# Softmax values of an attention layer: how many query groups are transposed by DMA, and where the softmax sums are divided out

## The chip, the cores and the metric

The kernel runs on one core of a Trainium2 chip. The metric is the device time of one execution in microseconds (us). The engines are TensorE (PE, with its weight loads PEld), VectorE (DVE), ScalarE (ACT), GpSimd (POOL) and SyncE (SP, which here only issues DMAs).

## The reference, cut to what matters

Four layers on x of 4 x 1024 x 256 in fp32, each added to x: a linear recurrent layer, a gated sparse feed-forward layer (ffn), attention with 8 heads of 64, and the same ffn again. The change is in the attention layer:

```python
q = (x @ Wq.T).reshape(b, t, 8, 64)
kv_latent = x @ Wkv_down.T
k = (kv_latent @ Wk_up.T).reshape(b, t, 8, 64)
v = (kv_latent @ Wv_up.T).reshape(b, t, 8, 64)
scores = jnp.einsum('bqhd,bkhd->bhqk', q, k) * 64 ** -0.5
attn = jax.nn.softmax(scores, axis=-1)
out = jnp.einsum('bhqk,bkhd->bqhd', attn, v).reshape(b, t, 512)
x = x + out @ Wo.T
```

x is layer-normalized before each layer. The weights Wk_up and Wv_up are folded into those of the queries and of the output, so that keys and values are both the latents of a batch (64 numbers for each of 1024 tokens).

## The kernel before, in words

**Stages.** The program has three stages after each other: the recurrent layer (c1 in the code), attention together with most of the first ffn (c2), and the second ffn (c3). In the attention part, the function `heads` is the main line, and `merge` (L952) places the steps of other generators between its steps, by due times counted in steps of `heads`. The instructions are recorded in this order, and then placed on the engines' queues by the builder with a model of their times (`schedule_with_timeline_sim`, L1298). Each engine works through its queue in order.

**The main line.** `heads` (L856) goes over 4 batches (one call for each, L1193), 2 blocks `nb` of 512 queries, 4 head pairs `g` and 4 groups `q` of 128 queries: 128 pairs of (group, head pair). A pair has two steps, one for each head `j`, which makes 64 steps a batch (`STEPS`). One step does this:

- scores (L881): four products of 128 x 512 on TensorE, high and low halves of the latents, into the PSUM buffer `sc`, 128 x 1024 (two buffers);
- the negated maximum `nm` (L885) on DVE, straight from `sc`;
- `pr` = exp(sc + nm) on ACT (L889, three buffers), which also sums each row into `ssum`.

Then the 128 x 1024 of `pr` have to be transposed, since the value product needs keys on the partitions. There are two ways:

- groups 0 and 2 (`by_dma`, L864): `nm` is shifted by 11 ln 2 on DVE (L887), ACT casts `pr` to fp16 (L892), POOL writes the remainder `pr - pd` as a second fp16 half (L893), and SP issues a DMA transpose of both halves, 128 x 2048 (L894), from `pd` (two buffers) into `d0` or `d1` (two buffers of each).
- groups 1 and 3: eight 128 x 128 transposes on TensorE (L900) into PSUM, and two copies of 128 x 512 by ACT (L905), or one by DVE (L903) in the last batch, into `p0` and `p1`.

**Value sums.** `values_sum` (L915) multiplies the transposed probabilities with the latents for both heads of a pair: 16 products in fp32 for the TensorE way (TensorE shows two instructions for each), 48 in fp16 for the DMA way, where each of 8 blocks of keys has three terms. They are called some steps later: that of a TensorE pair in the next pair's first step, that of a DMA pair in the second step of the next DMA pair. Each call also divides by the softmax sums: a reciprocal of `ssum` on DVE (L919), a broadcast of it to 64 columns a head on POOL (L921), a transpose of that on TensorE (L933), a copy to `rb` on ACT (L935), and a multiplication into `on` on DVE (L936). Its PSUM buffer `po` has the tag "s", of which there are two, shared with everything that `merge` places beside the main line.

**Output.** `output` (L938) runs for a block of 512 queries after its four head pairs, once for each of 4 groups: `on` for all heads (128 x 512) is split in a high half on ACT (L945) and a low half on POOL (L946), 12 products go to PSUM (L947), and DVE adds them to x (L948).

**Beside it.** `merge` also places 24 tiles of the first ffn (`Ffn.tile` with `fine=True`, in seven steps each), which use `ex`, `wk` and `xg` with two buffers each (L609, L610, L654); the queries (L842), the latents of the next batch (L782), and the second ffn's `head` (L501), which needs the x that `output` has written. After the main line, the last two groups' output and half a `head` run bare (L1194).

Of the kernel before, what the change touches and what calls it, by code (L numbers as in the profile page):

```python
# [487 lines left out]
class Ffn:  # L488
# [100 lines left out]
    def tile(self, i, sp, psum, tags, out=None, fast=False, parts=None, tt=None, fine=False):  # L589
# [18 lines left out]
        ssum = sp.tile([P, 2], F32, tag="ssum", name="ssum")  # L608
        ex = sp.tile([P, 2, D], F32, tag="ex", name="ex")  # L609
        wk = sp.tile([P, 2, D], F32, tag="wk", name="wk")  # L610
        for s in range(2):
# [161 lines left out]
class Attention:  # L773
    def __init__(self, tc, x, ident, ident64, wqk, wvo, wd, sp, wp):
        self.nc, self.x, self.ident, self.ident64 = tc.nc, x, ident, ident64
        self.wqk, self.wvo, self.wd, self.sp, self.wp = wqk, wvo, wd, sp, wp
        self.hp = None
        self.k, self.xnt, self.qs, self.on = {}, {}, {}, {}

        self.sident = wp.tile([HD, HD], F32R, tag="sident", name="sident")  # L780
# [74 lines left out]

    def heads(self, b, psum):  # L856

        nc, sp, wp = self.nc, self.sp, self.hp  # L860
        kh, kl, la, lb = self.k[b]
        late, pending = [], []
        for nb, g, q in ((nb, g, q) for nb in range(2) for g in range(PAIRS) for q in range(4)):
            by_dma = q % 2 == 0  # L864
            if g == 0:
                self.on[b, nb, q] = wp.tile([P, PAIRS, P], F32, tag=f"on{q}", name=f"on{q}")
            qs = self.qs[b, nb, g]
            ssum = sp.tile([P, 2], F32, tag="ssum", name="ssum", bufs=4)
            if by_dma:
                pts = [wp.tile([P, 2 * TPB, P], F16, tag=f"d{j}", name=f"d{j}", bufs=2) for j in range(2)]  # L870
                parts = ((0, lb[0]), (TPB, lb[0]), (0, lb[1]))
                terms = [(v[:, c, :], i + c) for c in range(TPB) for i, v in parts]
            else:
                pts = [wp.tile([P, TPB, P], F32, tag=f"p{j}", name=f"p{j}") for j in range(2)]
                terms = [(la[:, c, :], c) for c in range(TPB)]
            for j in range(2):
# [11 lines left out]
                pr = wp.tile([P, T], F32, tag="pr", name="pr", bufs=3)  # L888
                nc.scalar.activation(pr, sc, AF.Exp, bias=nm, accum_out=ssum[:, j : j + 1])  # L889
                if by_dma:  # L890
# [20 lines left out]
            (late if by_dma else pending).append((pts, terms, ssum, self.on[b, nb, q][:, g, :]))  # L911
        for args in late + pending:
            self.values_sum(*args, psum)

    def values_sum(self, pts, terms, ssum, on, psum):  # L915

        nc, sp = self.nc, self.sp
        rs = sp.tile([P, 2], F32, tag="rs", name="rs")
        nc.vector.reciprocal(rs, ssum)  # L919
        rows = sp.tile([P, 2, HD], F32, tag="rows", name="rows")  # L920
        nc.gpsimd.tensor_copy(rows, rs[:, :, None].to_broadcast([P, 2, HD]))  # L921
        po = psum.tile([P, 2, P], "s", "pmo")
        for n, (v, c) in enumerate(terms):
            for j in range(2):
                nc.tensor.matmul(  # L925
                    po[j * HD : (j + 1) * HD, 0, :],
                    v,
                    pts[j][:, c, :],
                    start=(n == 0),
                    stop=(n == len(terms) - 1),  # L930
                )

        nc.tensor.transpose(po[:, 1, :], rows.rearrange("p j d -> p (j d)"), self.ident)  # L933
        rb = sp.tile([P, P], F32, tag="rb", name="rb", bufs=1)
        nc.scalar.copy(rb, po[:, 1, :])  # L935
        nc.vector.tensor_tensor(on, po[:, 0, :], rb, ALU.mult)  # L936

    def output(self, b, nb, psum, tiles=range(4)):  # L938

        nc = self.nc  # L940
        for q in tiles:
            xt = self.x[b * TPB + nb * 4 + q]
            py = psum.tile([P, D], "s", "pmy")
            on = [self.hp.tile([P, PAIRS, P], F32R, tag=f"onp{i}", name=f"onp{i}") for i in range(2)]
            nc.scalar.copy(on[0], self.on[b, nb, q])  # L945
            nc.gpsimd.tensor_tensor(on[1], self.on[b, nb, q], on[0].bitcast(F32), ALU.subtract)  # L946
            products(nc, py, [([t[:, g, :] for t in on], [t[:, g, :] for t in self.wvo]) for g in range(PAIRS)])  # L947
            nc.vector.tensor_tensor(xt, xt, py, ALU.add)  # L948
            yield
# [79 lines left out]
def tile_kernel(ctx: ExitStack, tc: tile.TileContext, x_in, w_lru, vecs_in, rows, w_ffn, lin_t, w_attn, w_down, out):  # L1029
# [88 lines left out]
    with ExitStack() as c2:  # L1118
# [53 lines left out]
        for b in range(B):  # L1172
            n = STEPS * b
# [8 lines left out]
            side.append((n + 40 if b == B - 1 else n + STEPS + 24, f2.head(2 * b, sp, psum, "s"), 2))  # L1182
            last = b == B - 1
            side.append((n + STEPS if last else n + STEPS + 8, f2.head(2 * b + 1, sp, psum, "s", (0,) if last else (0, 1)), 1 if last else 2))
# [117 lines left out]
```

## Time and profile before

| What | us |
|---|---|
| median of 3 runs | 1536.99 (1534.27 to 1539.68) |
| the profiled execution's own time | 1533.81 |
| its span | 1532.1 |
| busy in the span: PE, PEld | 1297.4, 960.2 |
| busy in the span: DVE, ACT, POOL | 1182.9, 1014.5, 681.6 |
| DMA transposes | 128, on the queue q1 with 88.50 MB |

The span is cut in 40 slices of 38.3 us below. A digit is the busy share of an engine in a slice in tenths, and 9 is 90% or more; PEclk is the clock granted to TensorE in tenths of full speed.

```
PE   4879998698898898898998889888999998657786
[...]
DVE  8976665697887878887778687777676675499998
ACT  5353433664787777787787777877777776476664
[...]
PEclk9999999698999999999999999999999999789888
DMA  3010000331454334344433345434444454000000
```

The attention stage with its DMA transposes runs from slice 11 to slice 34. A row of a group by line has the line, engine, operation, what it writes and reads, shapes and count; then busy time and the mean duration of one in ns; then the engine's idle time just before, with what ended most of it. A row of the waits has who waited for whom, and then the total in us, how many times, and the longest. A row of the busy times by stretch has, for each engine, its busy us and in brackets its number of instructions.

### The profile page before, as it was taken

What the parts mean: (1) busy time and instruction counts of PE and PEld (TensorE: products, weight loads), DVE (VectorE), ACT (ScalarE), POOL (GpSimd) and SP (SyncE); (2) the same over time, 40 slices, a digit from 0 to 9 for tenths busy, and PEclk for the clock granted to TensorE, in tenths of its full rate; (3) what the DMA queues carried; (4) which work ended last, traced back from release to release, by engine and by line L of the source; (5) the groups of instructions that cost most, each with busy time, mean ns of one, the idle gap of its engine ahead of it and who ended that gap; (6) DMA issues with size and microseconds to landing.
All of it is one profiled execution on the core that took longest, in us unless ns stands there. A gap on an engine that the chain in (4) does not pass through costs nothing. (4 is left out here: it accounts for less than half of the span.)

```text
span 1532.1 us, 28693 instructions
## 1 busy us (share of the span) xinstructions
PE 1297.4 (85%) x10136; PEld 960.2 (63%) x10136; DVE 1182.9 (77%) x3674; ACT 1014.5 (66%) x2145; POOL 681.6 (44%) x848
## 2 busy tenths in 40 slices
PE   4879998698898898898998889888999998657786
PEld 3635455365676766766776767677777776334554
DVE  8976665697878887878778687777676675499998
ACT  5353433664787777787777787877777776476664
POOL 2033333162545454544543554454443534157776
PEclk9999999698999999999999999999999999789888
DMA  3010000331454334344433345434444454000000
GB/s 117 32 41 15 21 21 14 135 101 44 76 91 90 70 70 80 67 80 77 85 76 60 65 85 81 66 60 85 78 75 88 83 95 83 1 11 24 25 25 28
DMA packets 288609, 96.51 MB, mean 63 GB/s; under 512 B 268233, under 2 KB 284626, under 8 KB 288466
## 3 DMA queue, kind: packets, MB, share of 16 engines
q1 hardware_dynamic: 283024, 88.50, 29.0%
q10 hardware_dynamic: 5442, 6.18, 1.2%
q8 instruction: 80, 1.31, 0.3%
q14 instruction: 63, 0.52, 0.1%
HBM read 16.01 MB, written 11.53 MB: 18 GB/s over the span
## 5 line engine op out<-in xcount | busy, mean ns | idle before, releaser
L893 POOL TENSOR_TENSOR pd<-pr,pd 128x1024 f16<-128x1024 f32 x128 | 273.5, 2142 | 256.5 <-ACT pd L892 198.6
L885 DVE TENSOR_REDUCE nm<-sc 128x1 f32<-128x1024 f32 x256 | 308.5, 1218 | 76.8 <-PE sc L881 75.3
L889 ACT ACTIVATE pr<-sc,nm 128x1024 f32<-128x1024 f32 x256 | 285.9, 1120 | 89.8 <-DVE nm L887 53.3
L881 PE MATMUL sc<-kh,qs 128*128 128x512 f32 x512 | 184.9, 439 | 27.1 <-ACT pr L889 19.5
L881 PE MATMUL sc<-kl,qs 128*128 128x512 f32 x512 | 162.4, 398 | 0.0
L674 DVE MATCH_REPLACE8 wk<-m,wk 128x256 f32<-128x256 f32 x384 | 158.3, 419 | 0.1
L905 ACT COPY p<-ptp 128x512 f32<-128x512 f32 x224 | 124.3, 590 | 46.3 <-PE ptp L900 38.2
L900 PE MATMUL ptp<-ident,pr 128*128 128x128 f32 x1024 | 140.2, 277 | 15.6 <-ACT pr L889 14.8
L674 DVE MAX8 m<-wk 128x8 f32<-128x256 f32 x384 | 153.0, 424 | 0.4
L925 PE MATMUL pmo<-p,la 128*64 128x128 f32 x2048 | 142.3, 287 | 5.6 <-ACT ft L524 2.9
L900 PEld LDWEIGHTS ptp<-ident,pr 128*128 128x128 f32 x1024 | 117.1, 141 | 38.0 <-ACT pr L889 24.9
L892 ACT CAST pd<-pr 128x1024 f16<-128x1024 f32 x128 | 133.3, 1055 | 5.9 <-DMA d<-pd 4.8
L925 PEld LDWEIGHTS pmo<-p,la 128*64 128x64 f32 x2048 | 121.5, 143 | 24.2 <-ACT ft L524 5.1
L881 PEld LDWEIGHTS sc<-kh,qs 128*128 128x128 f32 x512 | 85.6, 196 | 51.9 <-ACT pr L889 30.8
L881 PEld LDWEIGHTS sc<-kl,qs 128*128 128x128 f32 x512 | 97.1, 190 | 23.4 <-issue 1.4
L925 PE MATMUL pmo<-d,lb 128*64 128x128 f16 x3072 | 101.8, 221 | 7.6 <-DVE qs L853 2.5
L925 PEld LDWEIGHTS <-lb 128*64 128x64 f16 x3072 | 91.2, 111 | 25.4 <-issue 19.5
L628 POOL TENSOR_TENSOR ex<-ex,wk 128x512 f32<-128x512 f32 x61 | 77.6, 1273 | 50.8 <-DVE wk L674 41.7
L921 POOL COPY rows<-rs 128x128 f32<-128x128 f32 x128 | 36.2, 295 | 125.5 <-PE pmo L933 69.3
L936 DVE TENSOR_TENSOR on<-pmo,rb 128x128 f32<-128x128 f32 x128 | 36.5, 285 | 66.8 <-ACT rb L935 66.2
L699 PE MATMUL pf<-wf,vt 128*128 128x256 f32 x288 | 84.4, 438 | 3.6 <-ACT vt L697 3.6
L147 PE MATMUL pt<-ident,xn 128*128 128x128 f32 x256 | 48.2, 308 | 42.5 <-ACT xn L145 30.6
(306 smaller groups left out, 2789.0 us busy)
## 6 DMA issues: line engine op xcount, KB each, us to landing
tt<-ft SPq DMA_DIRECT2D x16, 256.0 KB
tt<-tt SPq DMA_DIRECT2D x8, 512.0 KB
out<-x SPq DMA_DIRECT2D x32, 128.0 KB
x<-in_x ACTq DMA_DIRECT2D x6, 512.0 KB
pf<-pfs SPq DMA_DIRECT2D x12, 256.0 KB
full<-pf SPq DMA_DIRECT2D x24, 128.0 KB
d<-pd SPq DMA_TRANSPOSE x128
wa<-in_w_attn SPq DMA_DIRECT2D x2, 640.0 KB
```

The costliest lines, as they stand in the source:

```text
L147: nc.tensor.transpose(pt[:, k, i * P : (i + 1) * P], xn[:, k * P : (k + 1) * P], ident)
L628: pool.tensor_tensor(ex, ex, wk, ALU.subtract)
L674: ins = make(*args).ins
L699: nc.tensor.matmul(dst, vt[:, k, :], w.wf[:, k, :], start=(k == 0 and bias is None), stop=(k == KD - 1))
L881: nc.tensor.matmul(sc[:, sl], qs[:, j, q * P : (q + 1) * P], kk[:, sl], start=(i == 0), stop=(i == 1))
L885: nc.vector.tensor_reduce(nm, sc, AX.X, ALU.max, negate=True)
L889: nc.scalar.activation(pr, sc, AF.Exp, bias=nm, accum_out=ssum[:, j : j + 1])
L892: nc.scalar.copy(pd[:, 0, :], pr)
L893: nc.gpsimd.tensor_tensor(pd[:, 1, :], pr, pd[:, 0, :], ALU.subtract)
L900: nc.tensor.transpose(pt[:, kk, :], pr[:, kc * P : (kc + 1) * P], self.ident)
L905: nc.scalar.copy(dst, pt)
L925: nc.tensor.matmul(po[j * HD : (j + 1) * HD, 0, :], v, pts[j][:, c, :], start=(n == 0), stop=(n == len(terms) - 1),)
```

## The change

- Groups 0, 1 and 2 of each four go through the DMA transpose; group 3 stays on TensorE. `d0` and `d1` get a third buffer; `pd` keeps two, `pr` three.
- The ffn tiles beside attention hold `ex`, `wk` and `xg` in one buffer each.
- A DMA pair's value sum is called in a second step once two such pairs wait for it.
- `values_sum` no longer divides: ACT copies the raw sums from PSUM into `on`. The softmax sums of all 8 heads of a group are kept in `sums` (two buffers for each group). `output` makes one reciprocal of 8 columns, a broadcast to 128 x 512 on POOL (in the buffer of the low half, `onp1`), four transposes on TensorE into one PSUM buffer "s", and one multiplication of 128 x 512 on DVE, as a step of its own.
- `heads` is one generator over all batches; sums that wait at the end of a batch go on into the next.
- Due times: a step of `output` follows the last after 0.7 instead of 1.5 or 1; a few starts move by half a step to two steps.

```diff
-        ex = sp.tile([P, 2, D], F32, tag="ex", name="ex")
-        wk = sp.tile([P, 2, D], F32, tag="wk", name="wk")
+        one = {"bufs": 1} if fine else {}
+        ex = sp.tile([P, 2, D], F32, tag="ex", name="ex", **one)
+        wk = sp.tile([P, 2, D], F32, tag="wk", name="wk", **one)
...
-        xg = sp.tile([P, D], F32, tag="xg", name="xg", bufs=2)
+        xg = sp.tile([P, D], F32, tag="xg", name="xg", bufs=1 if fine else 2)
...
-        for nb, g, q in ((nb, g, q) for nb in range(2) for g in range(PAIRS) for q in range(4)):
-            by_dma = q % 2 == 0
+        for b, nb, g, q in (
+            (b, nb, g, q) for b in range(B) for nb in range(2) for g in range(PAIRS) for q in range(4)
+        ):
+            kh, kl, la, lb = self.k[b]
+            by_dma = q < 3
             if g == 0:
                 self.on[b, nb, q] = wp.tile([P, PAIRS, P], F32, tag=f"on{q}", name=f"on{q}")
+                self.sums[b, nb, q] = sp.tile([P, HEADS], F32, tag=f"ssum{q}", name=f"ssum{q}", bufs=2)
...
-                pts = [wp.tile([P, 2 * TPB, P], F16, tag=f"d{j}", name=f"d{j}", bufs=2) for j in range(2)]
+                pts = [wp.tile([P, 2 * TPB, P], F16, tag=f"d{j}", name=f"d{j}", bufs=3) for j in range(2)]
...
-                nc.scalar.activation(pr, sc, AF.Exp, bias=nm, accum_out=ssum[:, j : j + 1])
+                h = 2 * g + j
+                nc.scalar.activation(pr, sc, AF.Exp, bias=nm, accum_out=self.sums[b, nb, q][:, h : h + 1])
...
-                if j == 1 and late and by_dma:
+                if j == 1 and len(late) > 1:
                     self.values_sum(*late.pop(0), psum)
...
-    def values_sum(self, pts, terms, ssum, on, psum):
-        nc, sp = self.nc, self.sp
-        rs = sp.tile([P, 2], F32, tag="rs", name="rs")
-        nc.vector.reciprocal(rs, ssum)
-        rows = sp.tile([P, 2, HD], F32, tag="rows", name="rows")
-        nc.gpsimd.tensor_copy(rows, rs[:, :, None].to_broadcast([P, 2, HD]))
-        po = psum.tile([P, 2, P], "s", "pmo")
+    def values_sum(self, pts, terms, on, psum):
+        nc = self.nc
+        po = psum.tile([P, P], "s", "pmo")
...
-        nc.tensor.transpose(po[:, 1, :], rows.rearrange("p j d -> p (j d)"), self.ident)
-        rb = sp.tile([P, P], F32, tag="rb", name="rb", bufs=1)
-        nc.scalar.copy(rb, po[:, 1, :])
-        nc.vector.tensor_tensor(on, po[:, 0, :], rb, ALU.mult)
+        nc.scalar.copy(on, po)
 
     def output(self, b, nb, psum, tiles=range(4)):
...
+            rs = sp.tile([P, HEADS], F32, tag="rs", name="rs")
+            nc.vector.reciprocal(rs, self.sums[b, nb, q])
+            rows = self.hp.tile([P, HEADS, HD], F32, tag="onp1", name="rows")
+            nc.gpsimd.tensor_copy(rows, rs[:, :, None].to_broadcast([P, HEADS, HD]))
+            pb = psum.tile([P, PAIRS, P], "s", "pmr")
+            for g in range(PAIRS):
+                nc.tensor.transpose(
+                    pb[:, g, :], rows[:, 2 * g : 2 * g + 2, :].rearrange("p j d -> p (j d)"), self.ident
+                )
+            on = self.on[b, nb, q]
+            nc.vector.tensor_tensor(on, on, pb, ALU.mult)
+            yield
...
-            side.append((n + 33, at.output(b, 0, psum), 1.5))
-            side.append((n + STEPS - 1 if b == B - 1 else n + STEPS + 1.5, at.output(b, 1, psum, range(2 if b == B - 1 else 4)), 1 if b == B - 1 else 1.5))
+            side.append((n + 33, at.output(b, 0, psum), 0.7))
+            side.append((n + STEPS - 1 if last else n + STEPS + 1, at.output(b, 1, psum, range(2 if last else 4)), 0.7))
...
-        merge(chain(*(at.heads(b, psum) for b in range(B))), side)
+        merge(at.heads(psum), side)
```

More of the change, by code (lines that the diff above doesn't have):

```diff
@@ L777, in __init__ @@
         self.hp = None
-        self.k, self.xnt, self.qs, self.on = {}, {}, {}, {}
+        self.k, self.xnt, self.qs, self.on, self.sums = {}, {}, {}, {}, {}
         self.sident = wp.tile([HD, HD], F32R, tag="sident", name="sident")
@@ L854, in queries, with heads @@
         yield
-    def heads(self, b, psum):
+    def heads(self, psum):
         nc, sp, wp = self.nc, self.sp, self.hp
-        kh, kl, la, lb = self.k[b]
         late, pending = [], []
-        for nb, g, q in ((nb, g, q) for nb in range(2) for g in range(PAIRS) for q in range(4)):
-            by_dma = q % 2 == 0
+        for b, nb, g, q in (
[3 more added lines that the diff above has]
+            by_dma = q < 3
             if g == 0:
                 self.on[b, nb, q] = wp.tile([P, PAIRS, P], F32, tag=f"on{q}", name=f"on{q}")
+                self.sums[b, nb, q] = sp.tile([P, HEADS], F32, tag=f"ssum{q}", name=f"ssum{q}", bufs=2)
             qs = self.qs[b, nb, g]
-            ssum = sp.tile([P, 2], F32, tag="ssum", name="ssum", bufs=4)
             if by_dma:
-                pts = [wp.tile([P, 2 * TPB, P], F16, tag=f"d{j}", name=f"d{j}", bufs=2) for j in range(2)]
+                pts = [wp.tile([P, 2 * TPB, P], F16, tag=f"d{j}", name=f"d{j}", bufs=3) for j in range(2)]
                 parts = ((0, lb[0]), (TPB, lb[0]), (0, lb[1]))
@@ L907, in heads @@
                     self.values_sum(*pending.pop(0), psum)
[L908 removed]
+                if j == 1 and len(late) > 1:
                     self.values_sum(*late.pop(0), psum)
                 yield
[L911 removed]
+            (late if by_dma else pending).append((pts, terms, self.on[b, nb, q][:, g, :]))
         for args in late + pending:
             self.values_sum(*args, psum)
[L915 to L922 removed]
+    def values_sum(self, pts, terms, on, psum):
+        nc = self.nc
+        po = psum.tile([P, P], "s", "pmo")
         for n, (v, c) in enumerate(terms):
@@ L925, in values_sum @@
                 nc.tensor.matmul(
[L926 to L930, printed above, removed]
-                )
-        nc.tensor.transpose(po[:, 1, :], rows.rearrange("p j d -> p (j d)"), self.ident)
-        rb = sp.tile([P, P], F32, tag="rb", name="rb", bufs=1)
-        nc.scalar.copy(rb, po[:, 1, :])
-        nc.vector.tensor_tensor(on, po[:, 0, :], rb, ALU.mult)
+                    po[j * HD : (j + 1) * HD, :], v, pts[j][:, c, :], start=(n == 0), stop=(n == len(terms) - 1)
+                )
+        nc.scalar.copy(on, po)
     def output(self, b, nb, psum, tiles=range(4)):
-        nc = self.nc
+        nc, sp = self.nc, self.sp
         for q in tiles:
             xt = self.x[b * TPB + nb * 4 + q]
+            rs = sp.tile([P, HEADS], F32, tag="rs", name="rs")
[10 more added lines that the diff above has]
+            yield
             py = psum.tile([P, D], "s", "pmy")
[L944 to L947, printed above, removed]
+            parts = [self.hp.tile([P, PAIRS, P], F32R, tag=f"onp{i}", name=f"onp{i}") for i in range(2)]
+            nc.scalar.copy(parts[0], on)
+            nc.gpsimd.tensor_tensor(parts[1], on, parts[0].bitcast(F32), ALU.subtract)
+            products(nc, py, [([t[:, g, :] for t in parts], [t[:, g, :] for t in self.wvo]) for g in range(PAIRS)])
             nc.vector.tensor_tensor(xt, xt, py, ALU.add)
@@ L1172, in tile_kernel @@
         for b in range(B):
-            n = STEPS * b
+            n, last = STEPS * b, b == B - 1
             side += [
@@ L1179, in tile_kernel @@
             ]
-            side.append((n + 33, at.output(b, 0, psum), 1.5))
-            side.append((n + STEPS - 1 if b == B - 1 else n + STEPS + 1.5, at.output(b, 1, psum, range(2 if b == B - 1 else 4)), 1 if b == B - 1 else 1.5))
-            side.append((n + 40 if b == B - 1 else n + STEPS + 24, f2.head(2 * b, sp, psum, "s"), 2))
-            last = b == B - 1
-            side.append((n + STEPS if last else n + STEPS + 8, f2.head(2 * b + 1, sp, psum, "s", (0,) if last else (0, 1)), 1 if last else 2))
+            side.append((n + 33, at.output(b, 0, psum), 0.7))
+            side.append((n + STEPS - 1 if last else n + STEPS + 1, at.output(b, 1, psum, range(2 if last else 4)), 0.7))
+            side.append((n + 40 if last else n + STEPS + 24, f2.head(2 * b, sp, psum, "s"), 2))
+            side.append((n + STEPS + 2 if last else n + STEPS + 8, f2.head(2 * b + 1, sp, psum, "s", (0,) if last else (0, 1)), 1 if last else 2))
             if b < B - 1:
```

## The prediction

> **What bounds the kernel now.** I read the page first, then the busy times by stretch, the groups by line, the waits, and last a few microseconds of the timeline with the DMA packets. The slices of the page show three stages. The change touches only the middle one, which runs from the first score product (378 us) to the last value sum (1306 us):
>
> ```profile
> core 0: us, PE busy (x) PEld busy (x) DVE busy (x) ACT busy (x) POOL busy (x), PEclk, DMA share, GB/s
> 378.00:1306.00 928.00, 830.82 (x8355) 661.96 (x8357) 692.97 (x1723) 704.34 (x1373) 428.60 (x420) 0.98 0.43 77
> 1306.00:1532.00 226.00, 154.00 (x583) 100.86 (x579) 202.21 (x859) 134.24 (x407) 138.77 (x218) 0.82 0.06 19
> ```
>
> The reader is to see that TensorE is busy for 831 of 928 us here, ACT for 704, DVE for 693, POOL for 429, and the 16 DMA engines for 43%. TensorE is the bound, with about 97 us of gaps. The last stage is DVE's (202 of 226 us), and nothing in it changes. The stage is 32 rounds (4 batches, 2 blocks of 512 queries, 4 head pairs) of 8 steps (4 groups of queries, 2 heads): 928/32 = 29.0 us a round, 25.9 of it TensorE.
>
> The groups that the change removes or multiplies:
>
> ```profile
> L893 POOL TENSOR_TENSOR pd<-pr,pd 128x1024 f16<-128x1024 f32 x128 | 273.5, 2142 | 256.5 <-ACT pd L892 198.6
> L905 ACT COPY p<-ptp 128x512 f32<-128x512 f32 x224 | 124.3, 590 | 46.3 <-PE ptp L900 38.2
> L900 PE MATMUL ptp<-ident,pr 128*128 128x128 f32 x1024 | 140.2, 277 | 15.6 <-ACT pr L889 14.8
> L925 PE MATMUL pmo<-p,la 128*64 128x128 f32 x2048 | 142.3, 287 | 5.6 <-ACT ft L524 2.9
> L892 ACT CAST pd<-pr 128x1024 f16<-128x1024 f32 x128 | 133.3, 1055 | 5.9 <-DMA d<-pd 4.8
> L925 PE MATMUL pmo<-d,lb 128*64 128x128 f16 x3072 | 101.8, 221 | 7.6 <-DVE qs L853 2.5
> L921 POOL COPY rows<-rs 128x128 f32<-128x128 f32 x128 | 36.2, 295 | 125.5 <-PE pmo L933 69.3
> L936 DVE TENSOR_TENSOR on<-pmo,rb 128x128 f32<-128x128 f32 x128 | 36.5, 285 | 66.8 <-ACT rb L935 66.2
> ```
>
> Busy, not mean, is what counts for TensorE, since its instructions overlap. ACT almost never waits for the half-precision buffer pd (4.8 us in all), while DVE stands 66.2 us in the division of each value sum. The waits add one thing, who holds the SP queue:
>
> ```profile
> SPq L894 <- PE pmo L925: 189.6, 38, 14.3
> ```
>
> The transposes wait 38 times for the two d buffers. One pair of transposes in windows of 1 us:
>
> ```profile
> 787.00:788.00 1.00, 1.00 (x6) 0.78 (x5) 1.00 (x7) 0.81 (x2) 0.29 (x1) 1.00 0.03 5
> 788.00:789.00 1.00, 1.00 (x6) 0.84 (x5) 0.83 (x5) 1.00 (x3) 0.00 (x0) 1.00 1.10 211
> ...
> 792.00:793.00 1.00, 1.00 (x14) 0.96 (x15) 1.00 (x3) 0.84 (x3) 0.80 (x2) 0.96 1.05 197
> 793.00:794.00 1.00, 1.00 (x14) 1.00 (x12) 1.00 (x1) 1.00 (x2) 1.00 (x1) 0.50 0.06 17
> ```
>
> Two transposes fill all DMA engines from 788 to 793 us: 2.5 us each. From the packets of all 128: the first leaves 1.28 us after the issue, the last lands 2.72 us later. So one pd buffer is held, from the start of its cast to the landing, for at least 1.05 (cast) + 0.1 + 2.14 (POOL) + 4.0 = 7.3 us; measured median 7.34, mean 8.50 (the mean holds the waits for d).
>
> **What the Trainium skill says.** "Perfetto Trace Analysis", section Optimization Strategy: the same gap repeating on the engine that should be full can mean too few buffers. The trace agrees: of TensorE's own gaps, the largest are score products and transposes waiting for ACT's exp (19.5 and 14.8 us). "DMA: Bandwidth & Descriptors", section Anatomy of one DMA: a DMA's semaphore wait is spent on the issuing sequencer, not on the DMA engines. The trace agrees, with the 189.6 us on SP above. "TensorE: Matmul & The Clock Gate", section HAM oscillation, says that gaps of TensorE over about 3.4 us bring it back to half clock. The trace shows half clock (0.50 from 793 us) after TensorE was only 0.4 busy for two microseconds, so here shorter gaps go with it.
>
> **The change, part by part.** Busy time in the stage first.
>
> TensorE: the second of four groups leaves its path: 64 steps of 8 transposes, half of 140.2, -70.1. Its 32 value sums become half precision: -142.3/2 + 101.8/2 = -20.3. The 128 row transposes L933 become 4 for each of 32 output tiles, again 128: nothing. Sum -90: 831 becomes 740, 23.1 a round.
>
> ACT: 128 copies of 512 columns go, 112 of them ACT's at 124.3/224: -62. 64 casts come at 133.3/128: +67. The copy of rb becomes the copy of the value sum, same size (34.6): nothing. +5: 709, 22.2 a round.
>
> DVE: 64 shifts of nm (144 ns) +9; 16 copies of the last batch (684 ns) -11; reciprocals 128 to 32, -11; L936 -36.5; 32 multiplications 128x512 from PSUM at the 682 ns of row L161, +22. Sum -27: 666, 20.8 a round.
>
> POOL: 64 subtractions of 2.14, +137; L921 -36; 32 broadcast copies of 128x512, which the trace does not show: at least 0.3 (the small one), at most 1.28 (L946, two inputs); I take 0.9, +29. Sum +130: 558, 17.4 a round.
>
> DMA: 64 transposes of 2.5 us: +160 on about 400, 17.5 a round. SP issues 64 more of 2.09 us: 192 are 401 us of some 890, and the 22 loads of full stand in that queue between them; not a bound.
>
> No engine is over 23.1 now, but they also were not over 25.9 before, and the round took 29.0. So I take what the steps cost in this trace. From the starts of the 256 reductions L885, a DMA group takes 6.58 us (two steps) and a TensorE group 7.77. One group a round changes sides: -1.19. Three of four sums instead of two are short ones: TensorE 0.63 less, of which I count 0.4, as the intervals hold part of it. The divisions leave DVE's queue, where the reduction of the next scores stood behind 66.2 us of waits (2.1 a round). ACT's waits for nm are 80 us, so at most 2.1 may come back; at least nothing, as TensorE was the bound; I count 0.3. Three d buffers end most of SP's waits, which is no gain alone, but keeps pd from being held. Together 29.0 - 1.9 = 27.1.
>
> **What is late next: pd.** It keeps two buffers, and now six steps in a row need one instead of two in four. With a turnaround T, the fifth cast comes no earlier than 2T after the first, where the pace of 3.29 us a step would have it at 13.16. At T = 7.3 it is 1.4 late, at 7.8 (POOL fuller by 30%, two transposes meeting on the DMA engines) 2.4, at 8.5 3.8. A late cast blocks ACT's queue: behind it are the next exp, and behind that the score buffer and TensorE. The two steps without pd and the third pr buffer take up part of it: none at worst (2.4), all at best (0, since six casts need only 3T = 23.4 a round). I take 0.6: 27.7 a round, 1.3 x 32 = 42 us less.
>
> The single buffers for ex, wk and xg: one tile holds ex from 391.0 to 406.3 us in the trace, and tiles come every 6.75 steps, 23 us. I take nothing; at most two microseconds for each of 8 tiles of batch 0, whose steps overlap. The new due times place output and head steps otherwise among the 256 steps; the builder orders the queues itself, so the page can't tell what that does: from -5 to +5 us, taken as nothing. At the end two output tiles stand bare: reciprocal, copy, four transposes and a product for each (0.17 + 0.9 + 0.5 + 0.7 plus handoffs, about 2.5), of which rows and the low half share a buffer, so little overlaps; against it a rows and rb chain of 1.2 goes. +3, between 1 and 4.
>
> Sum -39 to -40 against the profiled execution's 1533.8 (span 1532.1), whose time is 0.2% under the median of 1537.0. The same difference from the median gives 1497 us.
>
> **Rivals.** (1) TensorE's relief arrives whole: pd's lateness is absorbed and DVE's waits come back: 26.2 a round, -90 + 3 = 1450. For it speaks that TensorE loses 90 us; against it that ACT then runs at 85% in order with three other engines. 0.12. (2) The pd ring decides and the time gets longer: nothing of the lateness is absorbed because ACT's order is fixed when the program is built. Then the round is 27.1 + 2T - 13.16, which passes 29.0 at T = 7.5; at T = 8.0 it is 29.9, +30 + 3, 1570. For it: the median of 7.34 is close to that point, and clustered casts. Against it: six casts fit in a round. 0.19. (3) The gain is eaten almost exactly, round 28.6 to 29.1, 1525 to 1543, since the loop scores, maximum, exp is not shortened. 0.14. (4) The forecast, 1470 to 1525: 0.55.
>
> **Numbers.** Differences under 0.3% (4.6 us) can't be told from none here. Faster: 0.55 + 0.12 + 0.05 of case 3 = 0.72; same 0.07; slower 0.19 + 0.02 = 0.21. The range leaves out about half of case 1 and half of case 2: 1450 to 1565; the likeliest case's own is 1470 to 1525.
>
> **What would show it.** Right: TensorE's busy time in the stage near 740, ACT's near 709, POOL's near 560; "ACT pd waits for DMA d" grown from 4.8 to some tens of us; SP's wait for pmo mostly gone; no DVE wait for rb; rounds near 27.7. Wrong: that ACT wait above 100 us and turnarounds over 8 us with TensorE clocks at half (rival 2), or hardly any such wait (rival 1), or output tiles that hold the two "s" buffers and new waits of pmo for them.

## The result, and the profile after

| | before | changed |
|---|---|---|
| median, us (lowest to highest) | 1538.34 (1534.27 to 1539.95) | 1680.97 (1676.47 to 1684.29) |
| ratio to before | | 1.093 [1.0895, 1.0964] |
| span of the profiled execution | 1532.1 | 1674.8 |
| first to last score product | 378.3 to 1294.8: 916.5 | 375.9 to 1422.5: 1046.6 |
| from the last score product to the end | 237.3 | 252.3 |

The changed kernel is 9.3% slower, 143 us. Of the 142.7 us in the span, 130 lie between the first and the last score product and 15 behind it; what precedes is 2 us shorter. First the busy times by stretch; the columns are those of the prediction's first fence (busy us and number of instructions of each engine, then TensorE's clock, the DMA share and GB/s).

```profile
core 0: us, PE busy (x) PEld busy (x) DVE busy (x) ACT busy (x) POOL busy (x), PEclk, DMA share, GB/s
380.00:1440.00 1060.00, 818.48 (x8364) 632.28 (x8364) 688.39 (x1574) 714.10 (x1326) 547.29 (x386) 0.92 0.49 99
1440.00:1675.00 235.00, 157.96 (x563) 103.76 (x562) 203.54 (x860) 133.63 (x406) 139.99 (x220) 0.78 0.06 19
```

No engine is busier than TensorE, and it stands still for 242 us of 1060 where it stood still for 97 of 928. Its busy time fell by only 12 us, but its clock fell too, from 0.98 to 0.92: busy time times clock went from 831 x 0.98 = 814 to 818 x 0.92 = 753. So, by this estimate, about 60 us of TensorE's work at full clock did go. Nothing came of it; the time between its instructions grew by more.

The groups by line (busy, mean ns of one, then the idle time just before them and what ended most of it):

```profile
L897 POOL TENSOR_TENSOR pd<-pr,pd 128x1024 f16<-128x1024 f32 x192 | 409.1, 2135 | 317.8 <-ACT pd L896 307.6
L884 PE MATMUL sc<-kh,qs 128*128 128x512 f32 x512 | 197.7, 469 | 104.0 <-ACT pr L893 86.6
L896 ACT CAST pd<-pr 128x1024 f16<-128x1024 f32 x192 | 200.2, 1047 | 128.2 <-DMA d<-pd 124.1
L925 PE MATMUL pmo<-d,lb 128*64 128x128 f16 x4608 | 172.9, 235 | 33.3 <-DMA d<-pd 9.2
L904 PE MATMUL ptp<-ident,pr 128*128 128x128 f32 x512 | 78.3, 296 | 14.2 <-ACT pr L893 13.3
L170 PE MATMUL pmy<-wvo,onp 128*128 128x256 f32 x384 | 66.7, 316 | 29.2 <-ACT onp L950 27.0
```

The counts are what the change says: 192 transposes by DMA, 4608 half-precision products, 512 transposes on TensorE. The durations are what they were (cast 1.05, remainder 2.14). What is new stands behind the bar. ACT's cast now waits 124.1 us for a pd buffer (4.8 before), and TensorE's score products wait 86.6 us for the exp that frees their buffer (19.5 before). The same waits, with how many and the longest, and SP's queue:

```profile
ACT pd L896 <- DMA d<-pd: 124.1, 80, 5.3
POOL rows L939 <- PE pmy L170: 34.3, 15, 3.8
...
SPq L898 <- PE pmo L925: 321.2, 39, 17.9
```

SP's waits for a d buffer, which the third buffer was to end, went from 189.6 to 321.2 us. The row of `rows` is the new one: POOL waits until TensorE has read the last tile's low half, since both use the buffer `onp1`. The transposes' hold on pd, from the start of the cast to the landing, has the same median as before, 7.34 us, and a longer mean, 9.13 against 8.50.

Where in the stage the time lies shows in the rounds (a head pair, four groups of queries), from the starts of the score products, as means over the blocks of four rounds:

| us | round 1 | 2 | 3 | 4 |
|---|---|---|---|---|
| before | 29.5 | 27.1 | 28.1 | 30.2 |
| changed | 26.2 | 43.1 | 31.3 | 30.5 |

The output tiles of a block begin in the first round of the next and run into the second, and it is the second that holds the loss. One of them, in the timeline (start, duration, engine, line, operation; in brackets the idle time before it and what ended it):

```profile
811.54 0.61 POOL L939 COPY rows<-rs 128x512 f32<-128x512 f32 x1
...
814.76 1.05 PE L942 MATMUL pmr<-ident,rows 128*128 128x128 f32 x4
...
816.21 0.68 DVE L946 TENSOR_TENSOR on<-on,pmr 128x512 f32<-128x512 f32 x1
816.39 0.63 PE L884 MATMUL sc<-kl,qs 128*128 128x512 f32 x2
816.80 0.15 DVE L890 TENSOR_SCALAR nm<-nm 128x1 f32<-128x1 f32 x1
816.92 0.62 ACT L950 CAST onp<-on 128x512 fp32r<-128x512 f32 x1 [1.45 <-DVE on L946]
...
817.68 1.27 POOL L951 TENSOR_TENSOR onp<-on,onp 128x512 fp32r<-128x512 f32 x1 [3.45 <-ACT onp L950]
...
819.01 1.46 PE L170 MATMUL pmy<-wvo,onp 128*128 128x256 f32 x10 [0.29 <-POOL onp L951]
...
820.60 0.61 POOL L939 COPY rows<-rs 128x512 f32<-128x512 f32 x1 [1.65 <-PE pmy L170]
...
821.50 12.06 SPq L898 DMA_TRANSPOSE d<-pd  x4
...
825.39 1.05 ACT L896 CAST pd<-pr 128x1024 f16<-128x1024 f32 x1 [1.90 <-DMA d<-pd]
...
828.67 1.04 ACT L896 CAST pd<-pr 128x1024 f16<-128x1024 f32 x1 [2.23 <-DMA d<-pd]
829.62 1.11 ACT L893 ACTIVATE pr<-sc,nm 128x1024 f32<-128x1024 f32 x1
...
830.87 1.22 PE L884 MATMUL sc<-kh,qs 128*128 128x512 f32 x2 [3.81 <-ACT pr L893]
```

Read it as one chain. A tile passes POOL, TensorE, DVE, ACT, POOL and TensorE, each step waiting for the last: 811.54 to 820.47. Only then may the next tile's `rows` start (820.60), because of the shared buffer. In TensorE's queue the half-precision value sums stand among these products, and a sum is what frees a d buffer. So SP's transposes begin only at 821.50, the pd buffers come free after that, and ACT's casts start at 825.39 and 828.67. The exp that is queued behind them starts at 829.62, though its shifted maximum was ready at 816.95. The scores behind that exp start at 830.87; those before ended at 817.02. Between them TensorE's main line stood for 13.9 us, while two output tiles went through.

### The profile page after: what moved, and what is told of

Same layout as the page of the kernel before. It is cut to its first block, busy times and chain, and to the rows that moved or that the text cites. A ratio compares the mean times of both kernels' runs of the same rounds, so it can differ in the third digit from the quotient of the medians.

```text
span 1674.8 us, 28633 instructions
## 1 busy us (share of the span) xinstructions
PE 1291.6 (77%) x10136; PEld 935.5 (56%) x10136; DVE 1180.3 (70%) x3530; ACT 1024.0 (61%) x2097; POOL 801.3 (48%) x816
## 4 chain that ended last, share of the span: by engine, by line
DVE 31%; PE 26%; ACT 13%; DMA 13%; POOL 9%; issue 7%; SPq 0%; ACTq 0%; POOLq 0%; DVEq 0%
DMA d<-pd 12%; DVE wk L675 8%; DVE m L675 6%; PE sc L884 5%; POOL pd L897 5%; DVE nm L888 5%; PE pmo L925 5%; ACT pr L893 4%; ACT pd L896 3%; PE po L437 2%; PE pu L170 2%; PE pmy L170 2%; PE pz L452 1%; PE ptp L904 1%; POOL ex L629 1%
## 5 line engine op out<-in xcount | busy, mean ns | idle before, releaser
L897 POOL TENSOR_TENSOR pd<-pr,pd 128x1024 f16<-128x1024 f32 x192 | 409.1, 2135 | 317.8 <-ACT pd L896 307.6
L896 ACT CAST pd<-pr 128x1024 f16<-128x1024 f32 x192 | 200.2, 1047 | 128.2 <-DMA d<-pd 124.1
L884 PE MATMUL sc<-kh,qs 128*128 128x512 f32 x512 | 197.7, 469 | 104.0 <-ACT pr L893 86.6
L925 PE MATMUL pmo<-d,lb 128*64 128x128 f16 x4608 | 172.9, 235 | 33.3 <-DMA d<-pd 9.2
L925 PEld LDWEIGHTS <-lb 128*64 128x64 f16 x4608 | 153.4, 120 | 67.6 <-issue 53.1
L884 PEld LDWEIGHTS sc<-kl,qs 128*128 128x128 f32 x512 | 105.2, 206 | 27.9 <-issue 3.1
L904 PE MATMUL ptp<-ident,pr 128*128 128x128 f32 x512 | 78.3, 296 | 14.2 <-ACT pr L893 13.3
L170 PE MATMUL pmy<-wvo,onp 128*128 128x256 f32 x384 | 66.7, 316 | 29.2 <-ACT onp L950 27.0
L170 PEld LDWEIGHTS pmy<-wvo,onp 128*128 128x128 f32 x384 | 59.0, 215 | 40.6 <-ACT onp L950 32.5
L904 PEld LDWEIGHTS ptp<-ident,pr 128*128 128x128 f32 x512 | 63.1, 151 | 31.8 <-ACT pr L893 20.3
L556 PE MATMUL pl<-lint,xc_f 128*128 128x512 f32 x128 | 75.7, 679 | 5.3 <-ACT xc_f L587 5.3
L147 PEld LDWEIGHTS pt<-ident,xn 128*128 128x128 f32 x256 | 33.0, 158 | 80.2 <-ACT xn L145 29.5
L700 PEld LDWEIGHTS pf<-wf,vt 128*128 128x128 f32 x288 | 61.0, 219 | 29.5 <-ACT vt L698 12.3
```

Source lines behind the costliest of these rows:

```text
L147: nc.tensor.transpose(pt[:, k, i * P : (i + 1) * P], xn[:, k * P : (k + 1) * P], ident)
L700: nc.tensor.matmul(dst, vt[:, k, :], w.wf[:, k, :], start=(k == 0 and bias is None), stop=(k == KD - 1))
L884: nc.tensor.matmul(sc[:, sl], qs[:, j, q * P : (q + 1) * P], kk[:, sl], start=(i == 0), stop=(i == 1))
L896: nc.scalar.copy(pd[:, 0, :], pr)
L897: nc.gpsimd.tensor_tensor(pd[:, 1, :], pr, pd[:, 0, :], ALU.subtract)
L904: nc.tensor.transpose(pt[:, kk, :], pr[:, kc * P : (kc + 1) * P], self.ident)
```

## The experiments

In the expectations, O is the theory that the output tiles with the division in them hold up the main line; D that the d buffers do; P that the pd ring does; A, formed later, that ACT and POOL, each in its order, do; and L, formed last, that the loop of the two score buffers (scores, maximum, shift, exp) sets the pace. R is D and P together; the other letters are explained where they stand. Times are medians in us, followed by the ratio to the kernel before with its 95% interval; diffs are cut (`...`) and are against the changed kernel unless said.

One thing limits all of them: the builder orders the queues anew for every edit. Counted in the traces by the place of each instruction between the scores, e6 below has the order of e1 throughout. But in e7 about a third of TensorE's other instructions in the stage stand at another step than in e1, and in e17 and e18 about half of them do against the kernels that they edit. So a difference is what an edit is worth together with the order that the builder makes of it. No run shows what the order is worth alone.

**The two halves of the change, each alone**

`e1_division_only` keeps two of four groups by DMA:

```diff
-            by_dma = q < 3
+            by_dma = q % 2 == 0
-                pts = [... tag=f"d{j}", name=f"d{j}", bufs=3) ...]
+                pts = [... tag=f"d{j}", name=f"d{j}", bufs=2) ...]
-                if j == 1 and len(late) > 1:
+                if j == 1 and late and by_dma:
```

> The changed kernel with two of four groups (0 and 2) on the DMA transpose again, two d buffers, and the value sum called as before; the division in the output, the single ex, wk and xg buffers and the due times stay changed. Theory D (the d ring: with three groups all three d buffers are taken, the third group's transpose waits for a value sum that is called one step ahead of it, and so holds pd and ACT): no loss here, 1500 to 1545 us. Theory P (the pd ring alone: two buffers, 7.3 us each): the same, 1500 to 1545. Theory O (the new output steps and their shared s buffers cost the time): 1590 or more.

Measured 1619.74, 1.0562 [1.053, 1.0593]. As O had it, and not D or P: more than half of the loss, 86 us, comes with no third group at all. `e5_all_but_division` is e1 with the division of the kernel before in `values_sum` and the output tiles spaced by 1.4 steps, since each is again one step; the single ex, wk and xg, the joined `heads` and the moved starts are kept:

```diff
-        nc.scalar.copy(on, po)
+        nc.tensor.transpose(po[:, 1, :], rows.rearrange("p j d -> p (j d)"), self.ident)
+        rb = sp.tile([P, P], F32, tag="rb", name="rb", bufs=1)
+        nc.scalar.copy(rb, po[:, 1, :])
+        nc.vector.tensor_tensor(on, po[:, 0, :], rb, ALU.mult)
...
```

> Two of four groups by DMA, two d buffers, and the division in each value sum as before; the single ex, wk and xg buffers, the one generator over all batches and the due times (1.4 for an output tile, which is one step here) as in the change. Theory O (the division moved to the output costs the 88 us of the division-only kernel): 1525 to 1550 us, as before the change. Theory E (the single ex, wk and xg buffers) or theory M (due times and the joined batches): 1590 or more.

Measured 1544.03, 1.0044 [1.0029, 1.006]: the edits that accompany the change cost about 7 us (0.3% to 0.6%). `e10_three_groups_old_division` is the kernel before with the third group:

```diff
-            by_dma = q % 2 == 0
+            by_dma = q < 3
-            ssum = sp.tile([P, 2], F32, tag="ssum", name="ssum", bufs=4)
+            ssum = sp.tile([P, 2], F32, tag="ssum", name="ssum", bufs=6)
-                if j == 1 and late and by_dma:
+                if j == 1 and len(late) > 1:
```

with three d buffers, and ex, wk, xg and rows in one buffer each for the room.

> Three of four groups by DMA with three d buffers, sums called once two pairs wait, ex, wk and xg single, but the division in each value sum as before the change (one rows buffer of 128x128 instead of two, six ssum), old due times, one call of heads for each batch. Theory G (the third group gains, as forecast, once the output tiles are as before): 1530 or less. Theory R (two pd buffers with 7.3 us a turn and d held by late sums cost more than TensorE's 90 us bring): 1560 or more, with over 80 us of ACT waits for the DMA.

Measured 1625.11, 1.0578 [1.0536, 1.062], as R had it. Each half alone costs 86 to 89 us, and both together 143, so some 32 us of their delays fall together. The timeline above shows a place where they meet, the output tiles that hold up the d and pd buffers of the third group; how much of the 32 us is there wasn't measured.

**What in the division costs: the shared buffer**

`e6_division_two_ex` is e1 with two buffers for ex, wk and xg; `e8_division_two_on` is e1 with two buffers of `on` for each group, so that a new block's sums needn't wait for the last block's output. The first is:

```diff
-        one = {"bufs": 1} if fine else {}
+        one = {}
-        xg = sp.tile([P, D], F32, tag="xg", name="xg", bufs=1 if fine else 2)
+        xg = sp.tile([P, D], F32, tag="xg", name="xg", bufs=2)
```

and the second:

```diff
-                self.on[b, nb, q] = wp.tile([P, PAIRS, P], F32, tag=f"on{q}", name=f"on{q}")
+                self.on[b, nb, q] = wp.tile([P, PAIRS, P], F32, tag=f"on{q}", name=f"on{q}", bufs=2)
```

> The division-only kernel (two of four groups by DMA, two d buffers, 1620 us) with two buffers for ex, wk and xg again. E: back to 1540 or less. O, M: 1600 to 1625.

> The division-only kernel with two buffers for each on tile instead of one. O2: the rounds after a block's end, 34 to 47 us long now, go to about 30, and the time at least 40 us lower, 1580 or less. O1, E: 1605 or more.

Measured 1618.27, 1.0526 [1.0477, 1.0575], and 1622.35, 1.0555 [1.0511, 1.0598]: neither does anything. `e7_division_own_rows` is e1 with a buffer for the broadcast:

```diff
-            rows = self.hp.tile([P, HEADS, HD], F32, tag="onp1", name="rows")
+            rows = self.hp.tile([P, HEADS, HD], F32, tag="rows8", name="rows")
```

> The division-only kernel with a buffer of its own for the broadcast reciprocals (rows), which shared that of the low half onp1. Theory O1 (the shared buffer strings the output tiles one behind another: rows of a tile waits for the last product of the tile before, 44 us of waits on POOL): the wait of rows for pmy gone and the time at least 40 us lower, 1580 or less. Theory O2 (on has one buffer for each group, and the next block's first sums wait until the longer output has read it): 1605 or more. E: 1605 or more.

Measured 1566.4, 1.0196 [1.0154, 1.0239]. With it 53 of the 86 us come back. An output tile follows the last (from one addition to x to the next within a block, the mean without the last block) after 5.84 us in the kernel before, 10.60 in e1, and 7.86 here. POOL's wait for the output product at the start of `rows` (46.6 us in e1) is gone. The last reader of `rows` itself stands in its place, and the wait for the reciprocal stays (23.1 us in the stage):

```profile
POOL rows L939 <- PE pmr L942: 17.6, 8, 6.7
```

`e9_changed_own_rows` makes the same edit in the changed kernel, and gives the ffn tiles' `full` one buffer instead of two for the room.

> The changed kernel, all of it, with a buffer of its own for rows; to make room, the ffn tiles' full has one buffer instead of two. Theory S (the shared buffer is the larger part of the loss, with three groups as with two): 55 us or more under the changed kernel, 1625 or less. Theory R (with three groups the ring of pd and d decides, and the output tiles only fill gaps): less than 25 us under it, 1655 or more.

Measured 1618.69, 1.0521 [1.0488, 1.0555]: 62 us of the 143 come back. The second round of a block falls from 43.1 to 33.7 us, and ACT's wait for pd from 124.1 to 92.1. The division left, e7's 30 us, was not taken apart further; 8 of them lie behind the last score product (245.4 us where 237.3 were).

**The d and pd buffers**

`e2_two_groups_three_d` is e1 with three d buffers; `e16_before_three_d` is the kernel before with three d buffers (and ex, wk, xg and rows single for the room).

> As the division-only kernel (two of four groups by DMA), but with three d buffers. D: SP's waits for pmo, 189.6 us before, fall under 60 us, and the time is within 1% of the division-only kernel, since pd has slack with two groups. P: the same time. O: as the division-only kernel, 1590 or more.

> The kernel before (two of four groups, old division) with three d buffers, and single ex, wk, xg and rows to make room. R: SP's 190 us of waits for pmo go, but pd has slack with two groups, so 0 to 12 us faster than before: 1524 to 1536. A: the same as before or up to 8 us slower, as the kernel with everything but the division.

Measured 1603.99, 1.0457 [1.0427, 1.0487], and 1542.62, 1.0042 [1.0024, 1.006]. In e16 SP's wait for the sums falls from 189.6 to 19.4 us and nothing is gained. So this wait cost nothing by itself there; where the output tiles delay the sums (e2) ending most of it (394.0 to 78.4 us) gives 16 us.

`e3_sum_one_pair_earlier` calls a DMA pair's sum one pair earlier in the changed kernel, so that its d buffers come free earlier. `e4_earlier_two_d_three_pd` is e3 with the buffers the other way round: two of d, three of pd. The first pair of lines is in both, the others in e4:

```diff
-                if j == 1 and len(late) > 1:
+                if j == 1 and late:
...
-                pts = [... tag=f"d{j}", name=f"d{j}", bufs=3) ...]
+                pts = [... tag=f"d{j}", name=f"d{j}", bufs=2) ...]
-                    pd = wp.tile([P, 2, T], F16, tag="pd", name="pd", bufs=2)
+                    pd = wp.tile([P, 2, T], F16, tag="pd", name="pd", bufs=3)
```

> The changed kernel, all of it, with one condition changed: in every second step the oldest waiting DMA value sum is called as soon as one pair waits (len(late) > 1 becomes late), so that d comes free one pair earlier. D: SP's waits for pmo fall from 321 us under 100, the mean hold of pd from 9.1 us to about 7.3, ACT's waits for the DMA from 124 us under 60, and the time to 1500 to 1570 us. P: pd still at 7 us a turn with two buffers, ACT's waits for the DMA stay over 90 us, the time 1600 to 1650. O: 1650 or more.

> As the kernel with the sum one pair earlier, but with two d buffers and three pd buffers (4 kB a partition less in all). D: with two d buffers each transpose waits for the sum of the pair before last, SP's waits for pmo go up again over 200 us, 1600 or more. P: ACT's waits for the DMA go under 30 us and the time is at least 40 us under that of the kernel with three d and two pd buffers. O: 1650 or more.

Measured 1651.32, 1.0761 [1.0726, 1.0796], and 1635.68, 1.0663 [1.0621, 1.0706]. Both help, by 26 to 30 and 41 to 45 us (by the ratios or the medians), and neither is near the kernel before. D had 1500 to 1570 for e3, P 1600 to 1650. In e3 SP waits 169.0 us for sums and ACT 75.5 for pd; in e4 it is 353.3 and 77.1. P's forecast for e4, ACT's wait under 30, failed: with a third pd in place of the third d, SP's wait doubled and ACT's stayed. A pd buffer isn't free until its transpose has landed, and the transpose waits for d.

`e11_three_old_division_three_pd` does what e4 does to e10; `e12_three_own_rows_three_pd` is e4 with own rows; `e15_own_rows_early` is e9 with the earlier sum.

> As the three groups with the old division, but with each waiting sum called one pair earlier, two d buffers and three pd buffers. R: ACT's waits for the DMA fall under 30 us and the time at least 20 us below that of the kernel with two pd and three d buffers. G, or a bound elsewhere: within 10 us of it.

> The kernel with earlier sums, two d and three pd buffers (1635.7 us) with a buffer of its own for rows. S: at least 45 us lower, 1590 or less. R, with d as its bound: 1610 or more.

> The changed kernel with its own rows buffer (1619 us) and the sums one pair earlier: three d, two pd. Theory R: SP's waits for pmo fall from 202 under 100 us, pd alone is left, 1575 to 1605. Theory A: 1605 or more.

Measured 1615.17, 1.0503 [1.0478, 1.0528]; 1595.36, 1.0379 [1.0354, 1.0404]; and 1604.49, 1.0444 [1.0419, 1.0469]. With one ring widened the other keeps its waits: e11 and e12 have little ACT wait for pd left (32.9 and 37.9 us) but SP waits of 221.6 and 299.9; e15 has 58.8 on SP and 71.1 on ACT. R had at least 20 us for e11, and 10 came (1625.11 to 1615.17); e12 fell between its two forecasts, and e15 came as R had it.

`e13_three_all_rings_wide` is e10 with the earlier sum, three d and three pd. The room comes from the first ffn's weight, which the tiles beside attention use whole in fp32 here, and not as a pair of halves. `e14_before_whole_weight` makes that last edit alone in the kernel before.

```diff
-            side.append((start, f1.tile(i, fp, psum, "sss", parts=wfs, fine=True), [1, 1, 1, 1, 1, 2, 1]))
+            side.append((start, f1.tile(i, fp, psum, "sss", fine=True), [1, 1, 1, 1, 1, 2, 1]))
```

> Three of four groups by DMA, old division, sums one pair earlier, three d and three pd buffers together; the room comes from the split ffn weight (wf in two halves), so the ffn tiles beside attention use the whole fp32 weight instead. Theory R (the two rings are what the third group costs): with both wide the gain of the third group shows, 1545 or less. Theory A (what is left is ACT and POOL in order: casts and subtractions in bursts that hold exp, whatever the buffers): 1570 or more.

> The kernel before with the whole fp32 ffn weight in place of its two halves beside attention, nothing else: the price of the room made in the kernel with all rings wide. Both theories: within 15 us of before, 1525 to 1550.

Measured 1574.89, 1.0247 [1.0226, 1.0268], and 1532.03, 0.9969 [0.9954, 0.9983]. Widening both rings brings back 50 us of e10's 89 (5 of them the weight's), where two d and three pd buffers with the same earlier sum (e11) brought 10. R, which had 1545 or less, missed; A had 1570 or more. Two rows of e13's waits in the stage, and one of SP's:

```profile
ACT pr L890 <- DVE nm L888: 98.5, 73, 5.3
ACT pd L893 <- DMA d<-pd: 27.9, 22, 3.6
...
SPq L895 <- PE pmo L926: 58.2, 10, 11.2
```

The rings are no longer what ACT waits for (27.9 us instead of 109.6 in e10). Yet with less TensorE work than the kernel before, this kernel is 2.5% slower. ACT waits for the shifted maximum instead.

**What paces a step: the score buffers' loop**

A score buffer is written, reduced, shifted (in a DMA step), read by exp, and written again two steps on. The table has the time from the start of a step's scores to the start of those two steps on, as the mean over both steps of a group, for groups 1 to 4 of a round (e17 and e18 follow below):

| us | group 1 | 2 | 3 | 4 | round |
|---|---|---|---|---|---|
| before (1 and 3 by DMA) | 7.04 | 7.02 | 6.98 | 7.71 | 28.7 |
| e18, before without shifts | 6.57 | 7.03 | 6.08 | 8.57 | 28.3 |
| changed (1 to 3 by DMA) | 6.41 | 7.06 | 8.20 | 11.21 | 32.9 |
| e13 (1 to 3 by DMA) | 7.00 | 6.35 | 7.00 | 9.59 | 29.9 |
| e17, e13 without shifts | 6.43 | 5.98 | 6.31 | 10.46 | 29.2 |

In the kernel before the two kinds of group take nearly the same time (7.01 by DMA, 7.36 by TensorE), though their work differs. That suggests a loop that both go through. Its means in the DMA steps of the kernel before: scores 1.32 us, 0.51 to the reduction, 1.2 of reduction, 1.44 from there to the exp with the shift in it, 1.11 of exp, and 1.41 to the scores two steps on: 7.0 for two steps. TensorE is part of this loop and not beside it: in the last link it is busy for 1.38 of the 1.41 us with other products. In the steps by TensorE that link is 2.52 us, TensorE being busy for 2.31 of them. In a part of e13's timeline the loop is stretched at one place:

```profile
710.63 2.12 POOL L894 TENSOR_TENSOR pd<-pr,pd 128x1024 f16<-128x1024 f32 x1
710.64 2.39 DVE L637 SCALAR_TENSOR_TENSOR full<-full,rs,ex 128x256 f32<-128x256 f32 x1
...
712.95 2.34 DVE L886 TENSOR_REDUCE nm<-sc 128x1 f32<-128x1024 f32 x2
...
715.22 0.26 DVE L888 TENSOR_SCALAR nm<-nm 128x1 f32<-128x1 f32 x2
715.45 1.11 ACT L890 ACTIVATE pr<-sc,nm 128x1024 f32<-128x1024 f32 x1 [5.28 <-DVE nm L888]
```

The small operation of the ffn on DVE, 0.47 us at its shortest, lasts 2.39 us, to within 0.3 us of the end of POOL's remainder beside it; two reductions and two shifts follow, and ACT has stood 5.28 us. The shift is the one link of the loop that can be left out by itself. In `e17_wide_rings_no_shift` (e13) and `e18_before_no_shift` (the kernel before) the probabilities then go to fp16 without the factor 2048:

```diff
-                if by_dma:
-                    nc.vector.tensor_scalar(nm, nm, PSHIFT * math.log(2.0), None, ALU.add)
```

> The kernel with all rings wide (1575 us) without the shift by 11 ln 2 of nm (192 instructions on DVE; the fp16 halves then hold probabilities up to 1 instead of 2048, so the small ones are rounded more coarsely). Theory L (the pace of a DMA step is the turn of the two score buffers: products, maximum, shift, exp, the products two steps on, 6.8 us for two steps, whatever TensorE has to do; the shift stands in this loop with a mean of 0.84 us from the end of the maximum to its start): 25 to 60 us lower, 1515 to 1550. Theory A (ACT and POOL in order hold the rest): less than 15 us lower, 1560 or more.

> The kernel before without the shift of nm in its 128 DMA steps, nothing else. L: the shift starts 0.75 us after the maximum's end there, so 15 to 45 us faster than before: 1490 to 1522. Where TensorE bounds the stage instead, as the forecast had it: within 8 us of before, 1528 or more.

Measured 1546.14, 1.0059 [1.0042, 1.0075], and 1519.36, 0.9876 [0.9858, 0.9893]. e17 is 29 us under e13 for 192 shifts, and e18 is 18 under its kernel before (1537.4) for 128: 0.15 and 0.14 us for each, and one lasts 0.144. Both are inside what L expected, near its lower ends, and outside what the others did. But that each shift brings just its own length is the net of two moves. In e18 two DMA steps take 0.68 us less (7.01 to 6.33), and two steps by TensorE 0.43 more (7.36 to 7.79); in e17 it is 0.54 less and 0.87 more. So DVE's instruction is on the path of the DMA steps, the steps by TensorE take part of the gain back, and the near equality of the two kinds goes with the shift. TensorE's work is about the same without the shift (busy time times clock is 739 in e13 and e17, and 806 and 801 in before and e18), so it wasn't a bound by itself in either. No run gave the loop a third score buffer or cut TensorE's work alone. e18 is faster than both kernels of the case, but it gives up the scaling of the probabilities ahead of fp16, so it is a measurement of the shift, not a free gain.

The sum of the third group, with the old division: 89 us. Both rings widened take off 45 (50 less the weight's 5), which leaves 44; e13 against e14 says 43. Of these, 64 more shifts of 0.15 are 10, as an estimate. The last 33 (e17 against e18 less the weight's 5 says 32) show as the fourth group's 9.6 to 10.5 us in e13 and e17, where 7.7 was before. There TensorE runs the transposes and a bunch of half-precision sums between an exp and the next scores: that link is 4.2 us in e13, TensorE being busy for 3.7 of them. Whether the order of the sums, POOL's hold on DVE, or both make this wasn't tried apart.

## Why the prediction was wrong

It said 1497 us, faster with 0.72, and a range to 1565; the chip said 1681, beyond its slower rival too. By its own steps:

**"TensorE is the bound".** This is the first failure, and the 61 us of gain (1.9 a round) rest on it. TensorE is the engine with the most busy time, but 831 of 928 us was read as a bound by itself, and a step is a chain through TensorE, DVE and ACT, 7.0 us for two steps. e18 shows it for the DMA steps, which got shorter by a cut on DVE; e13 shows it for the whole, slower by 43 us than e14 with less work for TensorE and both rings wide. The Trainium skill, "Perfetto Trace Analysis", section Identifying the Most-Contended Engine, says that matmul busy time is a poor measure of how near TensorE is to its peak. No run here measured that; what they show is that 60 us of its work went and the kernel got no faster.

**"-1.19 a round".** The prices of a DMA group (6.58) and a TensorE group (7.77) were cut at the starts of the first reduction of each group. Cut at the second reduction, the same trace gives 7.3 and 7.0, and cut at the first scores 7.0 and 7.4. Most of the difference came from where the cut was made, and wasn't a property of the two ways. No gain came of the -0.4 for shorter sums and the -0.3 for DVE's waits either; neither was tried alone.

**"Three d buffers end most of SP's waits".** They rose from 189.6 to 321.2 us. The prediction had counted the third buffer and not the third user: with the sum called once two pairs wait, three pairs need d at a time. With two users three buffers do end the wait (e16, 19.4), and with three they leave it where it was (e10, 178.9). The rest came with the output tiles, which with two groups and two d buffers raise it to 394.0 (e1). In the changed kernel the third group's transposes began 4.7 and 3.8 us after POOL's remainder on average for its two heads (0.7 to 1.8 in the first two groups). A wait of SP holds the source too: pd isn't free until its transpose lands.

**The pd ring, +0.6 a round.** The mechanism was right, rival 2 named it, and its sign came: ACT's wait above 100 us, at 124.1, with a clock down to 0.92. The size was taken with a turnaround of 7.8, and the mean is 9.13. But the rival's price, 1570, covers the ring alone. e10, which is the third group without the moved division, is at 1625, and e13 shows that the two rings together make 45 to 50 us of that. Fed with a mean hold of 9.13, the rival's rule gives 32.2 us a round, near the measured 32.7; but fed with e15's 6.97 it gives 27.9 where 30.4 was measured, so that nearness is luck.

**The moved division, costed at 0 for its due times and +3 for its tail.** Here is one of the two largest terms, with the third group's 89 us. The prediction saw that `rows` and the low half share a buffer, "so little overlaps", and charged it for the two bare tiles at the end alone. For the 30 other tiles it took the work as hidden beside the main line. It isn't: in the timeline above sums, transposes, casts and an exp follow on the tile's steps, each in its queue. e1 measures the division at 86 us, e7 against e1 the buffer at 53. The sign that it named for this, output tiles that hold the two "s" buffers and new waits of pmo for them, was near but not it: what is held is the d buffers, by the sums queued behind the output products. The stretch behind the last score product grew by 15 us where +3 stood. It comes with the division: it is 249.9 us in e1 and 239.7 in e10, where 237.3 were before.

**What held.** ACT near 709 (measured 707 from first to last score product), POOL near 558 (540). TensorE's work at full clock fell by about 60 instead of 90. DVE didn't lose 27 us: 685 against 687 before. The copy of 128x512 on POOL took 0.61 us, in the stated bounds of 0.3 and 1.28, with 0.9 taken; the multiplication took the 0.68 assumed. The single ex, wk and xg cost nothing (e6), as taken. DVE no longer waits for rb, as forecast, and no gain shows from it.

## What to carry to other kernels

A busy share of 90% doesn't make an engine the bound. Before work is taken off it, follow the ring of buffers that the main line goes through (here the two score buffers) link by link, and in each kind of step, since a gain in one kind can be taken back in the other. A price for a kind of step that changes with the point where the trace is cut isn't a price. A step that is spread over several engines' queues costs by what is queued behind it, so a scratch buffer shared between the first and the last operations of such a step strings one step after the other; here the shared buffer cost more than the rest of what the step added (53 of 86 us). Where two rings are held by one transfer (source and destination), count the users of both at once: with three groups, widening one left waits at the other, and widening both brought back half of the loss.

## What the runs showed of the hardware that was not expected

- DVE operations beside POOL's 2.14 us remainder are often stretched to about its length: L637 from 0.47 to 2.4 us and operations on 128x4 from 0.15 to 2.1. Of those stretched by over 0.5 us, 18 of 28 in the stage before lie beside a remainder, 20 of 30 in the changed kernel and 35 of 43 in e13. All excess of over 0.1 us above the shortest of the same line and shape sums to about 35, 43 and 54 us. The Trainium skill, "SBUF — State Buffer", section Who interferes with whom, says that a DVE instruction with two SBUF inputs contends with a GpSimd instruction that reads SBUF. The traces agree with such a hold for L637, which has two; no run here took POOL's part away to show it.
- The transposes moved their data faster in the kernels with the changed division: 2.03 us from the first packet to the landing, as a median, in the changed kernel, e1, e7 and e9, and 2.61 to 2.62 in before, e10, e13, e14, e17 and e18. Nothing tried here explains it.
- TensorE's mean clock was lower where it stood idle more: 0.98 with 10% idle in the stage before, 0.95 with 15% in e1, 0.94 with 18% in e13, 0.92 with 23% in the changed kernel. Part of the relief on TensorE is thus lost in busy time: busy 818 us at 0.92 for work that, by the estimate above, would be 753 at full clock.
